# A state-space block on one core: the gates of the last two groups move behind the scan, with the norm's scaling

## The chip, the cores and the metric

The kernel runs on one core of a Trainium2 chip. The time is the device time of one execution in microseconds (us). The time before is the median of three runs: 3396.68 us (3396.28 to 3397.22).

## The reference

Input x has 2048 tokens of 1024 channels, all in float32. After a layernorm over the channels (xn), the output is x + mixer(xn) + lora(xn). The lora part is a dense 1024x1024 layer and a routed low-rank one. The mixer matters here:

```
proj = xn @ in_proj_w.T                 # gate 4096 | x 4096, B 1024, C 1024 | dt 64
xBC  = silu(causal_conv4(x, B, C))      # four taps per channel
state = state * dA_t + dtx_t (x) B_t    # 64 heads of 64, 8 groups of 8 heads, 128 states
y_t  = state @ C_t + D * x_t
yn   = y * rsqrt(mean(y*y over the 512 channels of a group) + eps) * norm_weight
out  = (yn * silu(gate)) @ out_proj_w.T
```

So a group's gate (512 of the 4096 gate channels) and a group's root of the mean square meet y only at the end, just ahead of the output projection.

## The kernel before

Channels lie on partitions and tokens along the free axis. The two halves of the sequence (s = 0, 1; 1024 tokens each) and, within a half, two blocks of 512 tokens are the units of work.

*Products.* The input projection is computed by Strassen-like block products: two channel tiles form a `pair` (L488) that takes seven products in place of eight; one product is four matmuls of 128x128 by 512 columns, which the profile counts as eight. All pairs stand in one stream, `in_pairs` (L609): for each half and group three pairs for x, B, C, then, for groups from 2*NO on, two pairs for the gate (`g..`); at the end the pairs of the dense layer (`b..`). With NO = 3 these are groups 6 and 7. `stored` (L561) evicts a quarter of a pair and sends it to DRAM (`raw_d`, `gate_d`); the gate's quarters pass through Silu.

*Scan.* 32 blocks (half, group, half of the half) of four chunks of 128 tokens give 128 slots, in an order written out by hand. In each slot the program issues: one product; `scan_b` (L802) of this chunk (matmuls ps_y, ps_e, ps_st; on VectorE ecp times ps_e, the sum into xg, and the state update, whose decay GpSimd multiplies in first); `scan_a` (L740) of the next chunk in three steps (es on VectorE; ps_cb, cbm, the mask product into dab; the transposes ps_xt and the scalings xdt, xdd on ScalarE); between them the further products, with the convolution `conv` (L682) of the next block, layernorm of the second half, and sums of weights as side work. `plan` and `target` (L1075) spread the stream's products evenly over the slots. `pin` (L98) fixes the order of many VectorE instructions, and `keep_in_program_order` that of TensorE's.

*Norm.* At a block's last slot `norm_squares` (L867) squares xg on ScalarE and adds the four tiles on VectorE. In the next block's first slot `norm_mean` (L879) sums over the channels with a matmul of ones (ps_nv, PSUM bank "aux", the same as that of ps_cb), and ScalarE takes the root into `rms`; `norm_gate` (L887) takes the reciprocal (L890), scales xg by weight and root (L893), multiplies by the gate in groups 6 and 7 (L903), and stores to `y_d`.

*Gate stage.* Behind the scan, the gates of groups 0 to 5 are computed two groups at a time (an octet) by a two-level scheme: seven outer units of seven products each, 49 in place of 64, of matmuls with 256 columns (`ps_a_z`, `ps_x_z`, `ps_y_z`). `gate_units` (L1214) lists (half, octet, unit): 2 x 3 x 7 = 42. `left_two` makes weight sums on GpSimd, `oct_sums` those of an octet, `right_two` sums of activations on VectorE. As a quarter of an octet is complete, `gated` (L1299) loads y, takes Silu on ScalarE, multiplies on VectorE (L1310) and stores to `yg_d`; `later` puts its steps at given units and products.

*Output.* The output projection runs as a two-level scheme too (`ps_.._w`), with quarters loaded from `yg_d` or `y_d`.

All DMAs are issued on SyncE's queue (SP).

## Time and profile before

| | |
|---|---|
| median of three runs | 3396.68 us |
| the profiled execution, span | 3400.1 us |
| start, up to the scan's first slot | 0 to 181 us |
| scan, 128 slots | 181 to 2103 us |
| last products of the stream | 2103 to 2164 us |
| gate stage, 42 units | 2164 to 2685 us |
| output stage | 2688 to 3395 us |
| DMA | 799.38 MB, 235 GB/s |

The profiled execution is one run; the page gives no other time for it than its span, from its first to its last instruction, and what lies around the span is not in the table. Stages are told by the names of TensorE's tiles. In rows of the profile, L81 is the helper that issues every matmul and L85 the one for GpSimd; there one goes by the tile. Each float32 matmul counts as two. A matmul's duration holds its way through the array, so the pace is the distance from one to the next: 0.43 us for 512 columns.

### The profile page before, as it was taken

The page shows a single profiled execution, that of the slowest core. Times are in us where ns is not written, and L with a number is a line of the kernel's source. Part 1 is how long each engine was busy: PE and PEld are TensorE (multiplying, and loading weights), DVE is VectorE, ACT ScalarE, POOL GpSimd, SP SyncE. Part 2 cuts the span into 40 slices and gives each one's busy share as a digit, 9 for nine tenths or more (in the row PEclk, how much of TensorE's full clock was granted, in tenths as well). Part 3 has the DMA queues.
Part 4 walks back from the last instruction along what each step waited for, and adds up shares of the span by engine and source line. Part 5 has one row for each costly group of instructions (what it writes and reads, how often), then busy time and mean ns, then how long its engine had stood idle before and what let it go on. Part 6 is the DMA issues. An engine that isn't in the chain of part 4 may idle for free.

```text
span 3400.1 us, 41266 instructions
## 1 busy us (share of the span) xinstructions
PE 3344.5 (98%) x13828; PEld 2178.1 (64%) x13828; DVE 2489.8 (73%) x2688; ACT 1523.0 (45%) x4030; POOL 703.3 (21%) x499
## 2 busy tenths in 40 slices
PE   9999999999999999999999999999999999999999
PEld 7455554555555445555555554688888888888888
DVE  7479888878889988889888897455644565556554
ACT  2356666666666666666666664222222200000000
POOL 4122222222200021212112121474444100000000
PEclk9999999999999999999999999999999999999999
DMA  6657666656689988889898999677655787585654
GB/s 244 195 158 220 197 203 200 205 192 201 193 284 335 338 269 269 256 263 272 252 291 249 268 287 302 197 228 239 221 185 182 265 301 241 200 302 177 214 167 143
DMA packets 535571, 799.38 MB, mean 235 GB/s; under 512 B 34880, under 2 KB 264384, under 8 KB 531776
## 3 DMA queue, kind: packets, MB, share of 16 engines
q1 hardware_dynamic: 535360, 796.75, 72.8%
q8 instruction: 111, 1.82, 0.2%
q14 instruction: 100, 0.82, 0.1%
HBM read 546.00 MB, written 250.61 MB: 234 GB/s over the span
## 4 chain that ended last, share of the span: by engine, by line
PE 72%; DVE 14%; DMA 6%; ACT 5%; issue 3%; SPq 0%; POOL 0%; DVEq 0%; ACTq 0%; POOLq 0%
PE ps_x_x L81 10%; PE ps_x_w L81 8%; PE ps_y_x L81 6%; PE ps_a_x L81 6%; PE ps_y_w L81 5%; PE ps_a_w L81 5%; PE ps_x_z L81 5%; PE ps_y_z L81 3%; PE ps_a_z L81 3%; DVE xg L704 3%; PE ps_e L81 2%; PE ps_y L81 2%; PE ps_st L81 2%; PE ps_x_b L81 2%; DVE es L749 2%
## 5 line engine op out<-in xcount | busy, mean ns | idle before, releaser
L85 POOL TENSOR_TENSOR state<-state,tot 128x512 f32<-128x512 f32 x112 | 136.5, 1219 | 1085.0 <-PE ps_e L81 1003.3
L704 DVE SCALAR_TENSOR_TENSOR xg<-rawx,cw,xg 128x512 f32<-128x512 f32 x384 | 331.2, 870 | 9.6 <-ACT xg L698 2.3
L749 DVE TENSOR_TENSOR_SCAN es<-dab,here 128x1024 f32<-128x1024 f32 x128 | 296.1, 2313 | 10.8 <-ACT xdt L784 5.7
L81 PE MATMUL ps_x_w<-t,w 128*128 128x256 f32 x1344 | 303.8, 379 | 0.0
L767 ACT ACTIVATE ps_y<-xg,dsk 128x128 f32<-128x128 f32 x512 | 189.6, 370 | 207.3 <-DVE xg L832 182.6
L81 PEld LDWEIGHTS ps_x_w<-t,w 128*128 128x128 f32 x1344 | 255.4, 190 | 41.5 <-issue 7.4
L792 ACT ACTIVATE xdd<-xdt,es 128x64 f32<-128x64 f32 x1024 | 262.6, 392 | 1.4 <-DVE es L749 1.4
L784 ACT ACTIVATE xdt<-ps_xt,dt 128x64 f32<-128x64 f32 x1024 | 224.3, 337 | 62.7 <-PE ps_xt L105 62.7
L81 PE MATMUL ps_a_w<-q,w 128*128 128x256 f32 x896 | 202.7, 379 | 5.1 <-DMA w<-w 5.1
L1684 ACT COPY ps_x_w<-ps_a_w 128x512 f32<-128x512 f32 x28 | 16.0, 570 | 420.9 <-PE ps_a_w L81 420.9
L704 DVE SCALAR_TENSOR_TENSOR bc<-rawb,cw,bc 128x512 f32<-128x512 f32 x192 | 186.5, 977 | 20.8 <-ACT bc L698 17.3
L81 PEld LDWEIGHTS ps_a_w<-q,w 128*128 128x128 f32 x896 | 170.1, 190 | 28.8 <-issue 5.8
L81 PEld LDWEIGHTS ps_y<-dab,xdt 128*64 128x64 f32 x2048 | 112.4, 136 | 105.7 <-ACT xdd L792 83.9
L772 DVE TENSOR_TENSOR dab<-es,cbm 128x1024 f32<-128x1024 f32 x128 | 165.5, 1293 | 13.2 <-ACT cbm L760 12.8
L81 PE MATMUL ps_x_x<-op_again,s_x 128*128 128x512 f32 x384 | 172.7, 592 | 0.0
L81 PE MATMUL ps_a_x<-op_again,a_x 128*128 128x512 f32 x384 | 172.7, 592 | 0.0
L81 PE MATMUL ps_y_x<-op_again,s_x 128*128 128x512 f32 x384 | 172.7, 592 | 0.0
L81 PE MATMUL ps_x_x<-op,s_x 128*128 128x512 f32 x368 | 167.3, 598 | 0.9 <-ACT s_x L520 0.9
L81 PE MATMUL ps_y_x<-op,s_x 128*128 128x512 f32 x368 | 165.5, 592 | 0.0
L81 PE MATMUL ps_a_x<-op,a_x 128*128 128x512 f32 x368 | 165.5, 592 | 0.0
L81 PE MATMUL ps_y<-dab,xdt 128*64 128x128 f32 x2048 | 143.3, 279 | 7.6 <-ACT xdd L792 3.9
L831 DVE TENSOR_TENSOR ecp<-ecp,ps_e 128x512 f32<-128x512 f32 x120 | 81.8, 682 | 93.0 <-PE ps_e L81 88.2
(321 smaller groups left out, 6653.5 us busy)
## 6 DMA issues: line engine op xcount, KB each, us to landing
w<-w SPq DMA_DIRECT2D x196, 512.0 KB, 3.6
dab<-da_d SPq DMA_DIRECT2D x128, 512.0 KB, 6.7
raw<-ev SPq DMA_DIRECT2D x192, 256.0 KB, 4.2
a_x<-in_w_in_dram SPq DMA_DIRECT2D x168, 256.0 KB, 4.6
w<-wo SPq DMA_DIRECT2D x96, 448.0 KB, 4.8
ecp<-run_d SPq DMA_DIRECT2D x256, 128.0 KB, 5.9
y<-xg SPq DMA_DIRECT2D x64, 512.0 KB, 4.6
rawx<-raw SPq DMA_DIRECT2D x24, 1030.0 KB, 6.9
```

The costliest lines, as they stand in the source:

```text
L81: tc.keep_in_program_order(nc.tensor.matmul(*args, **kw))
L85: ins = nc.gpsimd.tensor_tensor(*args)
L704: ins = nc.vector.scalar_tensor_tensor(dst[:, i, :], raw[:, i, k : k + TB], cw[:, ti, k : k + 1], dst[:, i, :], ALU.mult, ALU.add,)
L749: ins = nc.vector.tensor_tensor_scan(es.rearrange("p h t -> p (h t)"), dab.rearrange("p h t -> p (h t)"), here, 0.0, ALU.mult, ALU.add,)
L767: nc.scalar.activation(psy[:, j, :], xg[:, j, cs], AF.Copy, scale=dsk[:, at : at + 1])
L772: nc.vector.tensor_tensor(ms, es, cbm.unsqueeze(1).to_broadcast([P, HG, Q]), ALU.mult)
L784: ins = nc.scalar.activation(xdt[:, h, :], x_t[:, h, :], AF.Copy, scale=dt_of[s][:, half * NQ + c, at : at + 1],)
L792: ins = nc.scalar.activation(xdd[:, h, :], xdt[:, h, :], AF.Copy, scale=es[:, h, Q - 1 : Q])
L831: pin(nc.vector.tensor_tensor(ecp, ecp, pse, ALU.mult))
L1684: nc.scalar.copy(px, pa)
```

## The change

NO goes from 3 to 4: the gates of all eight groups are computed in the gate stage, in 2 x 4 x 7 = 56 units. The stream holds no gate pairs, and `stored` no Silu and no delayed eviction. The norm is split. In the scan, xg is stored to `y_d` unscaled as soon as the block ends; the squares are summed over channels with the tokens on partitions (four matmuls with one column each), and a VectorE copy puts 4 values per partition into `msq`. After the last block `norm_roots` takes all roots and reciprocals at once, transposes them, and stores them to `rms_d`. In the gate stage `gated` loads y, loads the roots broadcast over the partitions (r), and scales y by weight and root on VectorE before the multiplication by the gate.

The order of a slot changes too. The second step of `scan_a` (ps_cb) comes before the slot's second product, the third (ps_xt) straight after it, and the rest of the products last; `conv` starts a slot earlier, with one or two steps in each slot. `oct_sums` of the two later octets both run in the gate stage, each in two units.

```diff
-NO = 3
+NO = 4
...
-                for q in range(2 if g >= 2 * NO else 0):
-                    t = 4 * g + 2 * q
-                    yield pair(
-                        f"g{g}_{q}", f"g_{s}_{g}_{q}", halves(w_in[t], w_in[t + 1]), ops,
-                        stored(gate_d[g], 2 * q, s, AF.Silu), s == 0,
-                    )
...
-    N_S = 5 * G - 4 * NO
+    N_S = 3 * G
...
+        nc.sync.dma_start(y_d[g][:, :, at : at + TB], xg)
...
-    def norm_mean(s, g, half):
-        y = y_of[s, g, half]
-        ps = ps_one.tile([P, TB], F32, tag="aux", name=f"ps_nv_{s}_{g}_{half}")
-        mm(ps, ones, y[:, 0, :], start=True, stop=True)
-        std = p1.tile([P, TB], F32, tag="rms", name=f"rms_{s}_{g}_{half}")
-        nc.scalar.activation(std, ps, AF.Sqrt, bias=eps, scale=1.0 / (4 * P))
...
+    def norm_sum(s, g, half):
+
+        y = sq_of.pop((s, g, half))
+        ps = ps_one.tile([P, NQ], F32, tag="aux", name=f"ps_nv_{s}_{g}_{half}")
+        for c in range(NQ):
+            mm(ps[:, c : c + 1], y[:, 0, c * Q : (c + 1) * Q], ones[:, 0:1], start=True, stop=True)
+        at = ((s * G + g) * 2 + half) * NQ
+        nc.vector.tensor_copy(msq[:, at : at + NQ], ps)
+
+    def norm_roots():
+
+        nc.scalar.activation(msq, msq, AF.Sqrt, bias=eps, scale=1.0 / (4 * P))
+        nc.vector.reciprocal(msq, msq)
+        ps = ps_one.tile([P, Q], F32, tag="aux", name="ps_roots")
+        transpose(ps, msq)
+        roots = const.tile([P, Q], F32, name="roots")
+        nc.scalar.copy(roots, ps)
+        nc.sync.dma_start(rms_d, roots)
...
+            if nxt:
+                if c == 0:
                     conv_steps = conv(*nxt)
-                parts[1] += steps(conv_steps, 1)
-                if c < 3:
                     parts[2] += steps(conv_steps, 1)
-                    tail = steps(conv_steps, 1)
+                elif c < NQ - 1:
+                    parts[1] += steps(conv_steps, 1)
+                    parts[2] += steps(conv_steps, 1)
+                else:
+                    parts[0] += steps(conv_steps, 1)
...
+            next(a, None)
             products(1, parts[1])
             next(a, None)
-            products(1, parts[2])
-            products(min(n - 3, 1), parts[3])
-            next(a, None)
-            do_put_off()
...
+            products(n - 2, parts[2])
...
+        r = gr.tile([P, 2, TB], F32, tag="gr", name=f"gr_{s}_{o}_{a}{n}")
+        nc.sync.dma_start(
+            r,
+            rows_d[s, 2 * o : 2 * o + 2, n * TB : (n + 1) * TB].unsqueeze(0)
+            .to_broadcast([P, 2, TB]),
+        )
...
+        for q in range(2):
+            for m in range(2):
+                t = 4 * (2 * o + q) + 2 * a + m
+                nc.vector.scalar_tensor_tensor(
+                    y[:, q, m], y[:, q, m], nw[:, t : t + 1], r[:, q], ALU.mult, ALU.mult
+                )
             yield
...
-            for du, n in ((1, 0), (1, 2), (1, 3), (after, 2), (after, 4)):
+            for du, n in ((1, 0), (1, 2), (1, 3), (1, 5), (after, 1), (after, 2), (after, 4)):
```

## The prediction

> **What bounds the kernel now.** I read the busy table of the page first, then busy time by stage, then one slot of the scan on the timeline, then the rows of the work that the change touches, and last the waits of TensorE and VectorE.
>
> ```profile
> PE 3344.5 (98%) x13828; PEld 2178.1 (64%) x13828; DVE 2489.8 (73%) x2688; ACT 1523.0 (45%) x4030; POOL 703.3 (21%) x499
> core 0: us, PE busy (x) PEld busy (x) DVE busy (x) ACT busy (x) POOL busy (x), PEclk, DMA share, GB/s
> 181.00:2103.00 1922.00, 1890.95 (x7529) 988.01 (x7531) 1682.66 (x1866) 1258.24 (x3603) 383.73 (x262) 1.00 0.80 248
> 2164.00:2686.00 522.00, 512.69 (x2352) 444.39 (x2350) 261.66 (x255) 146.47 (x223) 254.15 (x176) 1.00 0.62 207
> ```
>
> The first row is the page, the others are stages: 181 to 2103 is the scan, 2164 to 2686 the gate stage. TensorE has 31 us without work in the scan and 9 in the gate stage, so it sets the pace in both. But VectorE is 88% busy in the scan, and only 50% in the gate stage. The time of the change is therefore TensorE's work, plus whatever new idle time VectorE gives it. One slot shows how close the two are:
>
> ```profile
> 1622.39 1.16 PE L81 MATMUL ps_e<-bc,state 128*128 128x128 f32 x8
> 1623.38 1.02 PE L81 MATMUL ps_st<-xdd,bt 128*128 128x512 f32 x2
> 1623.59 0.69 DVE L831 TENSOR_TENSOR ecp<-ecp,ps_e 128x512 f32<-128x512 f32 x1 [2.62 <-PE ps_e L81]
> 1624.24 3.60 PE L81 MATMUL ps_y_x<-op_again,s_x 128*128 128x512 f32 x8
> 1624.91 0.68 DVE L846 TENSOR_TENSOR state<-state,ps_st 128x512 f32<-128x512 f32 x1
> 1625.51 2.28 DVE L749 TENSOR_TENSOR_SCAN es<-dab,here 128x1024 f32<-128x1024 f32 x1
> 1627.68 0.38 PE L81 MATMUL ps_cb<-bc 128*128 128x128 f32 x2
> 1631.44 0.60 PE L105 MATMUL ps_xt<-ident,xg 128*128 128x128 f32 x4
> 1635.41 1.09 PE L81 MATMUL ps_y<-dab,xdt 128*64 128x128 f32 x16
> ```
>
> (Start, duration.) A product is eight matmuls 0.43 us apart, 3.44 us. From the ps_y at 1621.37 to the next are 14.04 us: three products and 3.7 us of scan matmuls. The point to see is the order: ps_st, product, ps_cb, product, ps_xt, product. VectorE's ecp, sum into xg and state update have 7 us and more to finish before ps_xt, and ps_cb waits for none of them.
>
> ```profile
> L749 DVE TENSOR_TENSOR_SCAN es<-dab,here 128x1024 f32<-128x1024 f32 x128 | 296.1, 2313 | 10.8 <-ACT xdt L784 5.7 <-ACT xdd L792 5.0
> L890 DVE RECIPROCAL rms<-rms 128x512 f32<-128x512 f32 x32 | 106.7, 3334 | 11.7 <-ACT rms L884 11.7
> L893 DVE SCALAR_TENSOR_TENSOR xg<-xg,nw,rms 128x512 f32<-128x512 f32 x128 | 90.8, 767 | 0.0
> L81 PE MATMUL ps_nv<-sq,ones 128*128 128x512 f32 x64 | 32.7, 592 | 0.0
> DVE ecp L831 <- PE ps_e L81: 88.2, 41, 7.4
> PE ps_st L81 <- ACT xdd L792: 6.0, 11, 1.4
> PE ps_xt L105 <- DVE state L846: 5.3, 3, 2.5
> ```
>
> The fifth row is the key to the risk: VectorE waited for ps_e in only 41 of 120 slots. In the others it came to ecp late, with work queued from the slot before. The last two rows show how little of that lateness reached TensorE.
>
> **The change part by part.**
>
> *Products leave the scan.* The gate pairs of two groups are 2 x 4 pairs of 7 products: 56 x 3.44 = 192.6 us of TensorE less. The 128 slots then hold 343 products instead of 399: 87 slots of three and 41 of two (before: 113 of three, 15 of four). A slot of two lasts 14.04 - 3.44 = 10.6 us.
>
> *Gate stage grows by two octets of 49 products.* 42 units took 521.3 us (2163.7 to 2685.0), an octet of seven 86.9: +173.8 us. A two-level octet is cheaper than the 96.3 us of the same gates in one level (28 products x 3.44), by 9.4 us; this is all that TensorE gains, 18.8 us for both.
>
> *Norm in the scan.* VectorE loses 106.7 + 90.8 + 19.0 us (gate multiply) and 10.9 us of gate sums: 227 us, 1.8 us a slot, beside 1.5 us of products. ScalarE loses 62 table loads of 1.28 us and the 22 us of roots. None of this was TensorE's bound, so it is worth only the idle time it prevents. ps_nv becomes four matmuls of one column, eight weight loads: the nearest row is ps_e, eight loads in 0.97 us, against 2 x 0.43 now. 32 x 0.11 = +3.5 us.
>
> *The order in a slot, which costs most.* In the built order the products no longer lie between ps_st and ps_cb. It reads ps_st, (ps_nv), ps_cb, product, ps_xt, the rest. At each block's first slot ps_nv and ps_cb share one PSUM bank, and the reader between them is now a VectorE copy queued behind ecp, xg and state. By the slot above the state update ends 2.2 us after the start of ps_st; the copy (like the 0.16 us rows of 128x2) and a semaphore make it 2.5. ps_st and ps_nv end at 0.86 + 0.97 = 1.83. So TensorE waits 0.65 us per block, 32 x 0.65 = 21 us, and the whole lateness of VectorE comes on top. Behind the waiting copy stand es and the mask product; TensorE's queue holds everything else behind ps_cb.
>
> How late is VectorE? Its work from one ecp to the next, by the order and the rows: common part 2.05 (three of 0.68) + 2.31 + 1.29; slot 0 adds three convolution steps of bc at 0.98 (8.6 us), slot 1 three more and three of xg at 0.87 (11.2), slot 2 nine of xg (13.5), slot 3 the squares' sums 1.9 and, in the second half, four sums of wo of about 1.17 (12.2); and 0.5 for product sums in each. Against 14.04 it is on time; against 10.6 slot 2 runs 3.4 us over and slot 3 2.1. A third of the slots are such, spread evenly, so the copy comes about (3.4 + 12.7 - 14.04 = 2.1, 2.1 and 0)/3 = 1.4 us late in the second half. In the first half, with layernorm sums in place of wo, I take 0.5. These rows sum to 4% more than VectorE's busy time in the scan, so I cut to 0.9 and 0.35: 16 x 1.25 = 20 us. Where slot 2 was short, ps_xt of slot 3 also waits: it is due 4.7 us after ps_e, the state update ends 2.1 + lateness after it, so lateness over 2.6 costs; with the layernorm slots some 15 us. The sum is 56 us. Of the present 31, half of ScalarE's 18 goes with its table loads, and VectorE's share is replaced: 9 stay. Idle in the scan goes from 31 to 65: +34. Bounds: +5, if VectorE is early at every second block, and +75, if my rows are not cut and the product sums wait in its queue.
>
> *Gate stage, more VectorE work.* Four scalings per quarter at 767 ns, 16 per octet: 12.3 us on 40.6 of 86.9, so most is covered; but the sixth unit of each octet already has 10.6 to 12.4 us of VectorE in 12.6 to 14.1, and gets 3.1 more. Uncovered 1 us per octet: +8; bounds 0 and 24 (3.1 us each eight times). The broadcast of r (512 KB, like dab, 6.7 us to landing) is issued a unit's five products, 8.6 us, before its use, behind y's on SP: at nothing; a late one costs its delay up to 2 us. GpSimd's sums of the fourth octet, 16 more of 1.5 us, go under units where its own sums leave half of 12.1 us free.
>
> *One root for all* stands in TensorE's program order: copy, table load 1.28, root, reciprocal 0.95 (128x128 row of L345), transpose: +3 us once (0 to 5).
>
> **A rule of the skill against the trace.** The clock of 1.00 holds in nearly every stretch, but 690 to 700 us, after an idle gap of 2.1 us, was granted 0.83: 1.7 us lost. Three other gaps of 2.5 to 3.3 us lost nothing. Eight or so new gaps over 2 us at one in four: 8 x 1.7 / 4 = +3. The Trainium skill, "TensorE: Matmul & The Clock Gate", section "Part 1: The HAM clock gate", says that the clock falls to half only after an idle window of about 3.4 us; by it a gap of 2.1 us is harmless and this term would be 0. It speaks against any change that opens gaps; here the row shows that it can happen earlier.
>
> **Sum.** -192.6 + 173.8 + 3.5 + 34 + 8 + 3 + 3 = +32.7 us. The profiled execution has a span of 3400.1 us, 3.4 over the median of 3396.7, and I apply the difference to the median: 3429 us.
>
> **Rivals.**
> 1. *VectorE stays on time, and the change is faster.* With 1.8 us a slot off VectorE and its four slots evener, the copies come 0.65 us after need and no more: 21 + 9 idle, no growth: -192.6 + 173.8 + 3.5 - 1 + 3 = -13, so 3383. For it: VectorE's load per time falls in the scan, and 80 us of table loads go. Against: the wait for ps_e in only 41 slots, and short slots beside nine convolution steps. With a gate stage that hides its scalings, 12 us of growth in idle time bring it to zero.
> 2. *VectorE becomes the bound of short slots.* Growth +75, gate stage +24: -192.6 + 173.8 + 3.5 + 75 + 24 + 3 + 3 = +90, so 3486. For it: DVE at 88% now, product sums in its queue waiting for products. Against: a lighter sum per slot.
> 3. *Both cancel*: growth of 5 to 15 us and a gate stage that hides its scalings, 3392 to 3402.
> The change does do what it says: the built order holds eight octets and no gate pair in the scan.
>
> **Chances.** My case (growth 20 to 60, 3415 to 3455) 0.57; rival 1 0.15; rival 3 0.12; rival 2 0.16. Within 0.2% (about what a measurement of this kernel tells from no change, 6.8 us) falls most of rival 3: faster 0.15, same 0.10, slower 0.75. The range reaches halfway into rivals 1 and 2: 3390 to 3468.
>
> **What would show it.** Right: a new wait of PE ps_cb for the VectorE copy from ps_nv of 30 to 60 us in total, PE ps_xt on state above 10, a gate stage of 56 units near 703 us, a scan near 1922 - 189 + 34 = 1767. Wrong: ps_cb waiting under 15 us (rival 1), or gate units that last 13 us throughout.

## Result and the profile after

The changed kernel takes 3536.84 us (median of four runs, 3534.14 to 3538.66) beside 3396.48 us for the kernel before on the same chip: a ratio of 1.0417 (95% interval 1.0402 to 1.0432). It is slower by 140 us, where 32.7 were forecast. The profiled execution has a span of 3534.4 us, 134.3 more than that of before.

The busy row of the page, the kernel after:

```profile
PE 3371.4 (95%) x14357; PEld 2276.4 (64%) x14357; DVE 2442.2 (69%) x2733; ACT 1460.3 (41%) x3966; POOL 792.2 (22%) x555
```

Two numbers split the 134.3 us. TensorE's idle time, span less busy time, was 3400.1 - 3344.5 = 55.6 us and is 3534.4 - 3371.4 = 163.0: +107.4. Its busy time rose by 26.9 us, although by the rows of before its work fell by 15.3 (-192.6 + 173.8 + 3.5). So some 42 us are the same matmuls at half clock. The stages of the kernel after (window, length, busy time and count of each engine, granted clock, DMA):

```profile
178.00:2019.00 1841.00, 1736.95 (x7282) 932.45 (x7281) 1465.79 (x1713) 1146.25 (x3462) 359.99 (x246) 0.98 0.77 243
...
2082.00:2819.00 737.00, 695.42 (x3137) 598.47 (x3135) 443.56 (x457) 194.81 (x296) 368.40 (x248) 0.98 0.64 222
```

The first row is the scan: 104 us without work (31 before), although VectorE is less busy than before (1466 of 1841 us, 1683 of 1922 before). The second is the gate stage: 42 us without work (9 before), 737 us long instead of the 703 forecast. The clock was 1.00 in both before; 0.98 means that the scan ran 89 us and the gate stage 24 us at half speed (clock record of the trace).

What TensorE waited for, in the whole of the kernel after (total, times, longest):

```profile
PE ps_xt L105 <- DVE state L823: 46.5, 22, 9.5
PE ps_cb L81 <- DVE msq L857: 42.4, 30, 7.1
PE ps_x_z L81 <- ACT s_z L1379: 15.1, 11, 6.7
PE ps_x_z L81 <- DVE k L1361: 14.2, 6, 6.4
...
PE ps_roots L105 <- DVE msq L862: 3.6, 1, 3.6
```

The second row is the wait for the copy from ps_nv, the first the wait of the transposes for the state, 5.3 us before. By the two halves of the scan (178 to 1141 and 1141 to 2019 us) the second row falls into

```profile
PE ps_cb L81 <- DVE msq L857: 31.1, 14, 7.1
...
PE ps_cb L81 <- DVE msq L857: 11.3, 16, 2.1
```

In the second half most of these waits last 0.53 us, the price of the copy's place alone. The long ones stand in the first half: at 471, 661 and 848 us (4.8, 4.6 and 7.1 us) small instructions of the routing and of dt, lines 337 to 433, stand in VectorE's queue ahead of the copy, at 532 and 780 us (4.5 and 3.5 us) es and convolution steps.

The timeline shows how the first row's wait comes about, in a fourth slot that follows a short third one (start, duration):

```profile
944.01 6.79 DVE L681 SCALAR_TENSOR_TENSOR xg<-rawx,cw,xg 128x512 f32<-128x512 f32 x8
...
945.73 1.16 PE L81 MATMUL ps_e<-bc,state 128*128 128x128 f32 x8
...
946.73 1.02 PE L81 MATMUL ps_st<-xdd,bt 128*128 128x512 f32 x2
...
947.59 0.38 PE L81 MATMUL ps_cb<-bc 128*128 128x128 f32 x2
...
950.72 0.68 DVE L808 TENSOR_TENSOR ecp<-ecp,ps_e 128x512 f32<-128x512 f32 x1
...
952.11 0.68 DVE L823 TENSOR_TENSOR state<-state,ps_st 128x512 f32<-128x512 f32 x1
...
952.93 0.63 PE L105 MATMUL ps_xt<-ident,xg 128*128 128x128 f32 x4 [1.42 <-DVE state L823]
```

ps_e ends at 946.89, but VectorE has convolution steps of the slot before queued until 950.80 and reaches ecp 3.8 us late. The state update ends at 952.79, and ps_xt, which the new order puts one product behind ps_st, waits 1.42 us. Before, two products lay between them. Of the 46.5 us, 41.9 stand in slots that follow a short one.

The three longest of these waits are of another kind: ahead of ecp or of the state update VectorE was not busy but waited itself. Near the scan's end:

```profile
1947.66 5.28 POOL L85 TENSOR_TENSOR wo<-wo 128x512 f32<-128x512 f32 x4 [16.57 <-DMA wo<-in_w_out_dram]
...
1953.97 0.69 DVE L823 TENSOR_TENSOR state<-state,ps_st 128x512 f32<-128x512 f32 x1 [8.05 <-POOL state L85]
...
1954.71 1.12 PE L105 MATMUL ps_xt<-ident,xg 128*128 128x128 f32 x4 [9.52 <-DVE state L823]
```

The state's decay stood on GpSimd behind sums of wo that waited for their load. In the slots from 1032 and 1094 us (ps_xt waits 4.85 and 6.29 us) a convolution step of bc, ahead of ecp in VectorE's queue, waited 3.8 and 10.4 us for ScalarE, and weight sums stood between it and ecp. The second one:

```profile
1100.24 2.33 DVE L681 SCALAR_TENSOR_TENSOR bc<-rawb,cw,bc 128x512 f32<-128x512 f32 x3 [10.39 <-ACT bc L675]
```

These three make 20.7 of the 46.5 us.

### The profile page after: what moved, and what is told of

The parts are those of the page before. It is cut to its first block, busy times and chain, and to the rows that moved or that the text cites. A ratio compares the mean times of both kernels' runs of the same rounds, so it can differ in the third digit from the quotient of the medians.

```text
span 3534.4 us, 42377 instructions
## 1 busy us (share of the span) xinstructions
PE 3371.4 (95%) x14357; PEld 2276.4 (64%) x14357; DVE 2442.2 (69%) x2733; ACT 1460.3 (41%) x3966; POOL 792.2 (22%) x555
## 4 chain that ended last, share of the span: by engine, by line
PE 61%; DVE 17%; DMA 9%; issue 5%; ACT 5%; POOL 2%; SPq 1%; DVEq 0%; POOLq 0%; ACTq 0%
PE ps_x_x L81 9%; PE ps_x_w L81 8%; PE ps_a_x L81 6%; PE ps_y_x L81 5%; PE ps_a_w L81 5%; PE ps_y_w L81 5%; PE ps_x_z L81 5%; DVE xg L681 4%; PE ps_y_z L81 3%; PE ps_a_z L81 3%; DVE es L726 2%; PE ps_e L81 2%; PE ps_y L81 2%; PE ps_x_b L81 1%; DVE dab L749 1%
## 5 line engine op out<-in xcount | busy, mean ns | idle before, releaser
L85 POOL TENSOR_TENSOR state<-state,tot 128x512 f32<-128x512 f32 x112 | 128.1, 1143 | 1082.4 <-PE ps_e L81 960.9
L681 DVE SCALAR_TENSOR_TENSOR xg<-rawx,cw,xg 128x512 f32<-128x512 f32 x384 | 323.1, 853 | 7.1
L681 DVE SCALAR_TENSOR_TENSOR bc<-rawb,cw,bc 128x512 f32<-128x512 f32 x192 | 171.3, 893 | 36.0 <-ACT bc L675 33.6
L749 DVE TENSOR_TENSOR dab<-es,cbm 128x1024 f32<-128x1024 f32 x128 | 175.9, 1375 | 18.0 <-ACT cbm L737 14.3
L465 POOL TENSOR_TENSOR s_x<-a_x,a_x 128x512 f32<-128x512 f32 x48 | 72.4, 1507 | 400.8 <-PE ps_y_x L81 295.9
```

Of the source, the lines that this page charges most:

```text
L85: ins = nc.gpsimd.tensor_tensor(*args)
L465: nc.gpsimd.tensor_tensor(t[what], t[x], t[y], alu)
L681: ins = nc.vector.scalar_tensor_tensor(dst[:, i, :], raw[:, i, k : k + TB], cw[:, ti, k : k + 1], dst[:, i, :], ALU.mult, ALU.add,)
L749: nc.vector.tensor_tensor(ms, es, cbm.unsqueeze(1).to_broadcast([P, HG, Q]), ALU.mult)
```

## The experiments

Four questions: which part of the scan's idle time is the slot's order and which the short slots; whether gaps alone cost the clock; what lengthens the gate stage; and whether the parts can be mended. "Scan idle" is the length of the scan less TensorE's busy time in it, from windows cut at each run's own stage ends. All kernels start from the kernel after unless told otherwise; the kernel before took 3394.85 to 3397.52 us beside them. Short slots are those of two products, long ones those of three and four. Times are medians of four runs, e5 and e9 single ones; stages and waits are those of the one profiled run, whose time was the lowest of the four in e13 (3494 us) and at the upper end in e3, e17 and e18 (3538, 3509 and 3532 us).

### The scan: order or short slots

**e1_norm_late.** Moved:

```diff
-            if c == 0 and prev:
-                norm_sum(*prev)
...
             products(n - 2, parts[2])
+            if c == 0 and prev:
+                norm_sum(*prev)
```

> The changed kernel with one edit: the sum of squares (ps_nv and its VectorE copy) stands at the end of a block's first slot, behind its products, instead of between ps_st and ps_cb. Theory (the order opens the gaps: ps_cb waits for the copy): the 42.4 us that ps_cb waits for the copy fall below 5, a few half-clock stretches go with them, ps_xt's 46 us on the state stay or grow by 10 at most; 3537 becomes 3480 to 3505. Rival (VectorE is simply too slow for slots of two products): the time comes back at ps_xt on state and at ps_e, idle in the scan stays above 90 us, and the time above 3520.

Measured: 3504.25 us (ratio 1.0325, 1.0309 to 1.0342). The wait of ps_cb for the copy is gone; TensorE's waits in this run have two others:

```profile
PE ps_xt L105 <- DVE state L823: 58.0, 26, 13.5
...
PE ps_nv L81 <- ACT std L291: 12.0, 4, 4.7
```

So the copy's place was worth some 32 us of time. But scan idle fell by only 20 us, to 84 (the rest is TensorE's busy time, 11 us less, with the clock): part of the lateness moved to ps_xt, and ps_nv now meets the layernorm's sums in the same PSUM bank.

**e2_old_order.** The order of before in all slots:

```diff
             next(a, None)
-            next(a, None)
             products(1, parts[1])
             next(a, None)
             products(n - 2, parts[2])
+            next(a, None)
```

> The changed kernel with the slot's order of before: ps_st, product, ps_cb, the other products, ps_xt, in slots of two products too. Theory (order): the waits of ps_cb on the copy and of ps_xt on the state fall below 15 us together, scan idle goes from 104 to 25-45 us and its half clock from 89 to under 25 us; with the clock, 3537 becomes 3415 to 3450. Rival (two or three products a slot leave VectorE too little time): the same idle time turns up at ps_y or ps_e, scan idle stays over 70 us and the time over 3490.

Measured: 3497.49 us (1.0285, 1.0256 to 1.0315). Scan idle 72 us: the rival's case. By slots, idle in long slots fell from 84 to 26 us (29 in the slots of three before), but in the 41 short ones it rose from 20 to 47. There ps_xt stands right behind ps_cb, and from ps_cb to the next ps_y ScalarE has one product where it had two:

```profile
PE ps_y L81 <- ACT xdt L761: 23.6, 8, 7.5
...
PE ps_y L81 <- ACT xdd L769: 10.6, 7, 3.2
```

**e8_mid_order.** The old order in slots of three, the new one in slots of two:

```diff
-            next(a, None)
-            products(1, parts[1])
-            next(a, None)
-            products(n - 2, parts[2])
+            if n > 2:
+                products(1, parts[1])
+                next(a, None)
+                products(n - 2, parts[2])
+                next(a, None)
+            else:
+                next(a, None)
+                products(1, parts[1])
+                next(a, None)
+                products(0, parts[2])
```

> The changed kernel with the old order (ps_st, product, ps_cb, product, ps_xt) in the 87 slots of three products and its own order in the 41 slots of two. In e2 the old order took idle time in slots of three from 84 to 26 us but raised that of the short ones from 20 to 47. Theory (each kind of slot wants its own order): 26 + 20, scan idle 40 to 55 us, scan half clock under 55 us, time 3445 to 3475. Rival (lateness is only carried from slot to slot): scan idle 65 us or more, time 3490 or more.

Measured: 3511.84 us (1.0340, 1.0325 to 1.0356), scan idle 77 us. The two halves did not add up: slots of three stood at 47 us instead of 26. The rival held: the short slot ahead hands its lateness on.

**e4_before_no4.** The kernel before with four octets (and the sums' stores late, as in e3):

```diff
-NO = 3
+NO = 4
...
-            products(1, parts[2])
+            products(min(n - 2, 1), parts[2])
```

> The kernel before with the gates of all eight groups moved behind the scan (NO = 4, so that slots hold two or three products), but its own slot order, its own norm in the scan (reciprocal and scaling on VectorE, roots on ScalarE) and no scaling in the gate stage; the sums' stores stand late as in e3. Theory (order is what costs, not the number of products): 19 us fewer products, scan idle 30 to 60 us, little half clock: 3385 to 3425. Rival (short slots): VectorE has 1.8 us a slot more here than in the changed kernel, so scan idle above 100 us and the time over 3470.

Measured: 3491.29 us (1.0281, 1.0266 to 1.0296). The scan's window:

```profile
178.00:2007.00 1829.00, 1725.28 (x7091) 915.60 (x7088) 1654.20 (x1837) 1228.11 (x3545) 368.35 (x246) 0.99 0.79 244
```

1829 - 1725.28 = 103.7 us idle with the order and the norm of before: short slots alone, with the norm of before, bring as much idle time as the whole change. Theory (order) fell here. Against e2, which has short slots and the old order too, the lighter norm is worth some 31 us of idle time; the new order takes them back.

**e7_three_octets** and **e12_three_old.** The gate pairs of groups 6 and 7 are back in the stream; e12 has e2's order as well:

```diff
-NO = 4
+NO = 3
...
+                for q in range(2 if g >= 2 * NO else 0):
+                    t = 4 * g + 2 * q
+                    yield pair(
+                        f"g{g}_{q}", f"g_{s}_{g}_{q}", halves(w_in[t], w_in[t + 1]), ops,
+                        stored(gate_d[g], 2 * q, s), s == 0,
+                    )
```

> The changed kernel with NO = 3: the gate products of groups 6 and 7 are back in the scan, so slots hold three or four products as before, but slot order and norm are those of the change. Left out: these two groups' Silu, gate multiply and norm scaling. Theory A (the order opens the gaps): ps_cb waits on the copy 25 to 45 us and ps_xt on the state 20 to 45 us as in the changed kernel, scan idle 70 to 100 us, time 3450 to 3500. Theory B (slots of two products open them, since ScalarE and VectorE do not finish in 10.6 us): ps_cb under 25, ps_xt under 10, scan idle under 50 us, half clock in the scan under 25 us, time 3395 to 3440.

> e7 (NO = 3, three or four products a slot, the changed norm; Silu, gate multiply and scaling of groups 6 and 7 left out) with the old slot order. It fills the fourth field: new norm, old order, long slots. Theory (order and slot length add up): e7's 50 us of scan idle less the 32 of ps_cb, 18 to 30 us, half clock under 8 us, time 3405 to 3430. Rival (the new norm itself opens gaps): scan idle 40 us or more, time above 3440.

Measured: 3456.32 us for e7 (1.0180, 1.0161 to 1.0199), 3431.65 us for e12 (1.0107, 1.0092 to 1.0122). e7's waits:

```profile
PE ps_cb L81 <- DVE msq L864: 31.8, 31, 5.5
...
PE ps_xt L105 <- DVE state L830: 9.1, 6, 3.8
```

Neither pure theory held: ps_cb's wait stayed (order), ps_xt's all but went (short slots). With e12 the four fields are full (scan idle, us; time):

| | old order | new order |
|---|---|---|
| long slots (NO = 3) | e12: 28.8; 3431.7 | e7: 50.1; 3456.3 |
| short slots (NO = 4) | e2: 72.3; 3497.5 | after: 104.1; 3536.8 |

The order costs 21 to 32 us of idle time, the short slots 44 to 54; the short slots are the larger part. All four fields have the earlier start of `conv`. Waits of VectorE at bc for ScalarE come to 15 to 25 us of the scan in each of them, to 2.6 in the kernel before; no run tests this start by itself. (The times of the two rows differ by the gate stage too.) e12 is still 35 us behind the kernel before: 20 of them are its gate stage (542 us against 522), and its scan ran 24 us at half clock where under 8 were expected.

**e10_lean_conv.** One convolution tap less:

```diff
-                for k in range(1, KW):
+                for k in range(1, KW - 1):
```

> The changed kernel without the last tap of the convolution (left out: one of three multiply-adds of each tile, six of 0.87 us per block, 1.3 us of VectorE a slot; nothing else moves). Theory (VectorE's lateness in slots of two products): ps_xt on state falls from 46 to under 20 us, ps_cb on the copy to 20-28, scan idle from 104 to 45-65, its half clock from 89 to under 45 us, time 3537 to 3450-3480. Rival (the order alone sets the waits, however light VectorE is): scan idle stays above 85 us and the time above 3515.

Measured: 3502.20 us (1.0311, 1.0295 to 1.0328), scan idle 77 us, between the two cases. The waits tell why:

```profile
PE ps_cb L81 <- DVE msq L857: 41.9, 31, 5.8
...
PE ps_xt L105 <- DVE state L823: 22.8, 4, 11.6
```

With 153 us less VectorE time in the scan, ps_xt's wait halves, and ps_cb's does not move. What went from ps_xt is VectorE's lateness; of what is left, 11.6 us is again one wait for the decay on GpSimd. The second is the place of the copy, behind three instructions that need ps_e and ps_st: 0.53 us a block, in e7 too, and on top of it, in the first half above all, what stands ahead of the copy in VectorE's queue (31.6 us of waits in the first half, 10.4 in the second), much of it the routing's instructions, which this edit leaves as they are.

**e15_short_first.** All together:

```diff
-            n = target(slot) - done
+            if c == 0:
+                whole = target(slot + 3) - done
+            n = whole // 4 + (whole % 4 > (3, 2, 0, 1)[c])
```

with e1's place for `norm_sum`, e8's order and e14's gate stage.

> The changed kernel with all that the runs point to: the slots of two products are the first of each block (VectorE has 8.6 us of work there against 11 to 13.5 in the others), with nine more in second slots; they keep the new order, the slots of three have the old one; the sum of squares stands at its slot's end; gate stage as e14. Theory (short slots cost where VectorE has more work than the slot lasts): scan idle 104 to 25-45 us, its half clock under 30 us, the time 3425 to 3455; still behind the kernel before, since the gate stage and the clock take more than the 19 us of products saved. Rival (any short slot carries its lateness on): scan idle 60 us or more, time 3465 or more.

Measured: 3526.41 us (1.0389, 1.0372 to 1.0406), scan idle 76 us: by the numbers the rival. Its gate stage, built as e14's, took 754 us and lost part of the gain. But the scan is two different halves: in the second half of the scan idle fell to 16 us (34 in the kernel after, 5 in e12), in the first it was 61. There ps_nv at the end of the short slot waited 19.4 us for the layernorm's roots, and ps_xt 19.2 us for the state. That short slots are harmless where VectorE has little is thus borne out only where no layernorm runs.

### The clock: gaps made on purpose

**e5_gaps.** In the output stage of the kernel before, behind a unit's first product:

```diff
                     nc.scalar.copy(px, pa)
+                    held = w_ready[0][:, 0, 0:4, :]
+                    for _ in range(1 + (7 * t + units.index(i)) % 7):
+                        nc.scalar.copy(held, held)
```

> The kernel before, with one gap made on purpose in each of the 28 units of the output stage: behind the unit's first product ScalarE, after its copy of that product's sum, copies a part of the next product's weights onto itself once to seven times (0.58 us each by the ScalarE rows of the gate stage), and the next product waits for that. TensorE is otherwise without gaps there, so the clock record answers for each length alone. Theory (a gap near or over 3 us costs the clock): gaps under 2 us are followed by a half clock in at most 1 of 8, those over 3 us in at least 10 of 12, each by 3.4 us or more of half clock (1.7 us or more lost). Rival (the clock fell in the changed kernel for another reason, its many small matmuls): at most 3 of the 28 gaps are followed by one.

Measured: the output stage of 718 us has 9.9 us idle, as before: the copies depended on the weights alone and were put ahead of the product. No gaps, no answer.

**e9_gaps_held.** The same with the copies held behind the evicting copy:

```diff
-                    nc.scalar.copy(px, pa)
+                    ins = nc.scalar.copy(px, pa)
...
-                        nc.scalar.copy(held, held)
+                        one = nc.scalar.copy(held, held)
+                        behind(one, ins)
+                        ins = one
```

> As e5, whose gaps did not come about (the copies had been put ahead of the product that they were to follow): now each of ScalarE's one to seven copies of the next weights is held behind its copy of the first product's sum. By the 0.58 us rows the gaps are about 1.4 to 4.9 us, four of each length, in the output stage. Theory (gap length decides): under 2 us at most 1 of 8 followed by a half clock, over 3 us at least 10 of 12, 3.4 us or more of half clock each; some 12 to 18 half stretches in all. Rival (another reason): at most 3 of 28.

Measured: 28 gaps as planned, four each of 1.19, 1.90, 2.49, 3.14, 3.79, 4.44 and 5.09 us. Three of them on TensorE's timeline (in brackets the gap ahead of the row and what ended it):

```profile
2715.91 5.41 PE L81 MATMUL ps_y_w<-t,w 128*128 128x256 f32 x16 [1.90 <-ACT w L1687]
...
2806.97 6.43 PE L81 MATMUL ps_y_w<-t,w 128*128 128x256 f32 x16 [3.79 <-ACT w L1687]
...
2904.55 3.72 PE L81 MATMUL ps_y_w<-t,w 128*128 128x256 f32 x16 [1.19 <-ACT w L1687]
```

and windows around these three gaps (columns as in the stages above; the second last but one is the clock):

```profile
2713.50:2716.91 3.41, 1.51 (x8) 1.01 (x7) 3.31 (x3) 1.72 (x3) 0.00 (x0) 1.00 1.05 393
2716.91:2720.32 3.41, 3.41 (x10) 2.70 (x9) 0.70 (x1) 0.00 (x0) 0.00 (x0) 0.50 1.03 398
2802.25:2805.66 3.41, 0.93 (x5) 0.48 (x3) 2.29 (x1) 2.34 (x5) 0.00 (x0) 1.00 0.94 309
2805.66:2809.07 3.41, 2.10 (x5) 1.74 (x6) 0.00 (x0) 1.23 (x2) 0.00 (x0) 0.50 0.67 198
2809.07:2812.48 3.41, 3.41 (x9) 2.69 (x9) 0.00 (x0) 0.00 (x0) 0.00 (x0) 0.50 0.42 161
2901.24:2904.65 3.41, 2.22 (x11) 1.62 (x9) 2.91 (x3) 1.10 (x2) 0.00 (x0) 1.00 1.03 357
2904.65:2908.06 3.41, 3.41 (x16) 3.02 (x17) 3.33 (x2) 0.00 (x0) 0.00 (x0) 1.00 1.00 373
```

All 24 gaps of 1.90 us and more were followed by a half clock, the four of 1.19 us by none; 109 us of half clock in all. A gap of 1.90 us took 3.41 us of half clock, one of 3.79 us two such stretches. So gaps alone do it, without small matmuls, and earlier than theory had it. (All four gaps of 1.90 us lay within one window of the grid described at the end; in the kernel after two gaps of 1.97 and 1.98 us, at 711 and 646 us, cost nothing.) The stage grew by 140 us from its 715: 87 us of gaps and some 53 us of slow clock.

### The gate stage

**e3_stores_late.** The store step of the sums comes later:

```diff
-                for u, n in ((2 * k, 4), (2 * k + 1, 2), (2 * k + 1, 6)):
+                for u, n in ((2 * k, 4), (2 * k + 1, 2), (2 * k + 2, 3)):
```

> The changed kernel with one edit in the gate stage: the store step of GpSimd's operand sums of octets 3 and 4 is issued four products later (behind the third product of the next unit), so that SP has sent the next loads of y before it waits for GpSimd. Theory (SP's queue: y's load stands behind a store that waits for GpSimd): VectorE no longer waits for y, the six long units fall to about 13 us, the gate stage goes from 737 to about 705 us, the half clock in it from 24 to under 8 us, and 3537 becomes 3500 to 3512. Rival (VectorE's scalings, 3.1 us in a unit, are the cost): the gate stage stays above 725 and the time above 3525.

Measured: 3527.83 us (1.0397, 1.0378 to 1.0416), gate stage 745 us. By the numbers it is the rival, but the edit did not do what it was meant to: SP still waited 87 us for GpSimd at these stores (83 in the kernel after).

**e6_scale_late.** The scalings stand later:

```diff
-            for du, n in ((1, 0), (1, 2), (1, 3), (1, 5), (after, 1), (after, 2), (after, 4)):
+            for du, n in ((1, 0), (1, 2), (1, 3), (after, 1), (after, 2), (after, 3), (after, 4)):
```

> The changed kernel with one edit in the gate stage: VectorE's four scalings of a quarter stand three to four products later, all in the unit after next, so that none of them waits for y ahead of the sums of the unit before. Theory (a scaling whose y has not landed holds up the sums behind it in VectorE's queue): the wait of ps_x_z on k (14 us) and the six long units shrink, gate stage 737 to 705-718, time 3510 to 3522. Rival (3.1 us of VectorE work in crowded units is the cost, wherever it stands): the sixth and seventh units of an octet lengthen instead, gate stage 728 or more, time 3530 or more.

Measured: 3538.30 us (1.0419, 1.0404 to 1.0435), gate stage 742 us: the rival's numbers, and the theory's missed. But VectorE waited 72 us for y, longer than the 63 of the kernel after, and SP 92 us for GpSimd instead of 83, so the edit did not take that wait away.

**e11_pool_stores.** GpSimd issues the sums' stores (`queue` is `nc.gpsimd` for the sums of the gate stage):

```diff
-            nc.sync.dma_start(to[what], src)
+            queue.dma_start(to[what], src)
```

> The changed kernel with the 32 stores of the operand sums in the gate stage issued by GpSimd itself, behind its sums, so that SP's queue never waits for them; nothing else moves (e3 only moved that wait: SP still waited 87 us for GpSimd). Theory (y is late because SP stands at these stores): VectorE's waits for y fall from 63 to under 30 us, the long units shrink, gate stage 737 to 705-718, time 3508 to 3522. Rival (the scalings' own time, or y's transfers, are the cost): gate stage 730 or more, time 3528 or more.

Measured: 3526.70 us (1.0389, 1.0372 to 1.0406), gate stage 736 us. By the numbers the rival again, in its stage. SP no longer waits for GpSimd, but for the buffer of the next sums, whose loads it issues (10 us in the kernel after; window 2082 to 2400), and VectorE's wait for y fell only to 55 us:

```profile
SPq L886 <- DMA s<-ws: 63.2, 14, 15.1
```

The wait had moved once more.

**e13_no_sums.** Without the eight sums of the gate stage:

```diff
-            for k in range(8):
-                gen = oct_sums(gt, 2 + k // 4, k % 4)
-                for u, n in ((2 * k, 4), (2 * k + 1, 2), (2 * k + 1, 6)):
-                    later(u, n, lambda g=gen: next(g))
...
-                src = s_d[o][i][:, q]
+                src = s_d[o % 2][i][:, q]
```

> The changed kernel without GpSimd's operand sums of octets 3 and 4 in the gate stage, with their loads and stores (left out: these sums; the units of octets 3 and 4 read those of octets 1 and 2 in their place). e3, e6 and e11 only moved the wait of SP for GpSimd. Theory (the sums' loads and stores on SP make y late, and VectorE's scaling waits for y ahead of the next sums): the six long units go, all units are like those of the second pass in the changed kernel (35 units, 0.5 us over 12.09 each): gate stage 737 to 700-708, half clock there under 8 us, time 3500 to 3512. Rival (3.1 us of scalings in a unit are the cost): gate stage 725 or more.

Measured: 3501.24 us (1.0311, 1.0287 to 1.0335). The stage:

```profile
2075.00:2780.00 705.00, 685.31 (x3137) 592.26 (x3135) 426.41 (x457) 194.62 (x296) 302.33 (x216) 1.00 0.62 210
```

705 us with the scalings in it, at a clock of 1.00: with the scalings there, the sums of octets 3 and 4 cost 32 us, 22 of idle time and 10 of clock. Neither of the two is dear alone: by 521.3 + 173.8 the stage would last 695 us without both, with the scalings 705, with the sums alone (e4, stores late) 712; with both it is 737. And waiting for y is not what went: VectorE still waited 47.9 us for y in this stage (62.7 in the kernel after).

**e14_scale_z.** z is scaled in place of y, and r is loaded ahead of y, in a step of its own at `(0, 3)`:

```diff
-                    y[:, q, m], y[:, q, m], nw[:, t : t + 1], r[:, q], ALU.mult, ALU.mult
+                    z[:, q, m], z[:, q, m], nw[:, t : t + 1], r[:, q], ALU.mult, ALU.mult
```

> The changed kernel with the scaling applied to the gate z instead of y, and the root's rows loaded a unit earlier: VectorE does the same work at the same places, but no scaling waits for y; only the last multiply does, three to four products later. Theory (it is the wait for y ahead of the k sums, not the scalings' time): gate stage 737 to 708-718 (e4, without scalings and with the same sums, had 712), ps_x_z on k under 6 us, time 3508 to 3520. Rival (scalings' time): 730 or more, time 3528 or more.

Measured: 3551.83 us (1.0463, 1.0437 to 1.0488), gate stage 751 us: worse than either case. The early load of r waited on SP 76 us for its buffer, held by a scaling that now waits for Silu. The edit made a new wait and decides nothing.

**e16_no_adds** keeps the sums' loads and stores, **e17_no_transfers** their additions; both read `s_d[o % 2]` as e13 does:

```diff
-                gen = oct_sums(gt, 2 + k // 4, k % 4)
+                gen = oct_sums(gt, 2 + k // 4, k % 4, lambda *args: None)    # e16
...
+            def sums_only():                                                 # e17
+                a11, a12, a21, a22 = (held[:, j] for j in range(4))
+                add(a22, a21, a12, ALU.add)
+                add(a21, a11, a12, ALU.subtract)
+                add(a22, a21, a11, ALU.subtract)
+                add(a21, a12, a11, ALU.subtract)
+            for k in range(8):
+                later(2 * k + 1, 2, sums_only)
```

> As e13 (705 us of gate stage without the sums), but the sums' loads and stores stay and only GpSimd's 32 additions are left out (the stores carry the loaded quarters; octets 3 and 4 read the operands of octets 1 and 2). Theory A (SP's queue and the transfers): gate stage 720 us or more. Theory B (GpSimd's additions: SP's stores wait for them, and VectorE runs slower beside them): 703 to 712, time 3500 to 3512.

> As e13, but GpSimd's 32 additions stay, on a tile loaded once, and the sums' other loads and all stores are left out, so that nothing on SP waits for them. Theory A (SP's queue): gate stage 703 to 712. Theory B, in the part that VectorE runs slower beside GpSimd, or that the additions delay the units' own operands on GpSimd: 720 or more. If both e16 and e17 come out near 705, it is the stores on SP that wait for the additions, neither alone.

Measured: 3509.73 us for e16 (1.0335, 1.0320 to 1.0351), 3506.25 us for e17 (1.0322, 1.0306 to 1.0337). The gate stage of e16, without the additions:

```profile
2076.00:2795.00 719.00, 691.60 (x3137) 596.01 (x3135) 426.25 (x457) 195.15 (x296) 304.68 (x216) 0.99 0.65 219
```

and of e17, with the additions alone:

```profile
2077.00:2795.00 718.00, 691.23 (x3137) 595.47 (x3135) 448.16 (x457) 195.01 (x296) 364.36 (x248) 0.99 0.60 206
```

Against 705 us the transfers alone cost 14 us, the additions alone 13; together they make 32. The two small numbers are near the noise: the four runs of e13 lie between 3494 and 3511 us, and by the medians the transfers cost 8 us and the additions 5. That neither part alone makes the 32 us is clear of it: by the medians both together make 36. And the third busy column shows a part of how: VectorE's same 457 instructions take 426 us without GpSimd's 32 additions and 448 beside them.

**e18_spread.** A sum every two and a half units:

```diff
-                for u, n in ((2 * k, 4), (2 * k + 1, 2), (2 * k + 1, 6)):
+                for u, n in ((5 * k // 2, 4), (5 * k // 2 + 1, 2), (5 * k // 2 + 2, 3)):
```

> The changed kernel with the eight operand sums of the gate stage spread over 20 units instead of 16 (one every two and a half units, store step in the unit after the additions). Theory (the sums come too densely for SP and GpSimd): long units shrink to 13-17 us, gate stage 737 to 715-728, time 3516 to 3530. Rival (density does not matter, each sum costs its 4 us): 733 to 745, time 3530 or more.

Measured: 3521.31 us (1.0360, 1.0343 to 1.0377); gate stage 731 us, 6 less than in the kernel after, from the slowest of the four runs; the time fell by 16. Between the cases: density is a part, the smaller one.

No run points to a version that beats the kernel before: the best ones that compute everything are e4 with 3491 and e2 with 3497 us.

## Why the prediction was right or wrong

**Sign and kind of wait: right.** The change is slower, ps_cb waits for the copy from ps_nv, ps_xt for the state, as forecast; e1 and e10 show the two apart.

**The wait of ps_cb: the sum right by luck.** It was 42.4 us where the working had 21 + 20 = 41. The place alone was 0.53 us a block (0.65 taken). But the lateness on top was put at 0.35 us a block for the first half and 0.9 for the second, and it is the other way round: 31.1 us of waits stand in the first half (16 forecast), 11.3 in the second (25 forecast). In three of the first half's waits, 16.5 us together, it was the instructions of the routing and of dt, which the working's sum of a slot does not hold.

**Products, roots: right.** ps_roots waited 3.6 us (3 forecast). The gate stage without the sums of octets 3 and 4 took 705 us against 703: the scalings cost 10 us over 521.3 + 173.8, where 8 was taken.

**Failed: the term for ps_xt, "with the layernorm slots some 15 us".** It is 46.5 us, and with it scan idle grew by 73 us, from 31 to 104, where 34 was taken between bounds of 5 and 75. The step that erred prices the lateness of the state update from sums of VectorE's own work, averaged over slots. TensorE pays slot by slot, behind short slots above all (41.9 us), and 20.7 us of the wait are three cases in which VectorE itself waited, for ScalarE and for GpSimd; no term stood for that. For the same reason "the order in a slot, which costs most" is wrong: the fields show short slots at 44 to 54 us and the order at 21 to 32.

**Failed: the clock, "eight or so new gaps over 2 us at one in four ... = +3".** It was about 42 us. The kernel after has 18 gaps over 2 us, 17 of them followed by a half clock that lasts 3.4 to 10 us. All three factors were too small: before, four gaps were over 2 us, so 14 are new where eight were taken; one in four came from three harmless gaps of one trace, which by the grid described below each lay across two windows (0.94 + 1.59, 1.77 + 0.86 and 1.64 + 1.70 us); and 1.7 us is the price of the shortest stretch.

**Failed: "GpSimd's sums of the fourth octet go under units ...: at nothing" and "issued a unit's five products before its use ...: at nothing".** e13 puts the sums of octets 3 and 4 at 32 us beside the scalings, and e16 and e17 show that both their transfers and their additions are needed for it. Two chains are seen in the kernel after. In the first, SP's queue stands at a store that waits for GpSimd, y's load is issued behind it, VectorE's scaling waits for y, and the sums into k that TensorE's bank waits for (14.2 us) stand behind that scaling. From its windows 2082 to 2400 and 2078 to 2820:

```profile
SPq L895 <- POOL ws L85: 82.6, 32, 12.7
```

```profile
DVE gy L1269 <- DMA gy<-y: 62.7, 23, 6.8
```

The second is as long, 15.1 us, and goes over ScalarE:

```profile
2210.77 2.83 DVE L1269 SCALAR_TENSOR_TENSOR gy<-gy,nw,gr 128x512 f32<-128x512 f32 x2
...
2213.52 3.35 DVE L1279 TENSOR_TENSOR c<-c,k 128x2048 f32<-128x2048 f32 x1
...
2216.90 1.06 ACT L1264 ACTIVATE c<-c 128x1024 f32<-128x1024 f32 x1 [8.12 <-DVE c L1279]
...
2220.01 3.75 PE L81 MATMUL ps_x_z<-op_again,la 128*128 128x256 f32 x8 [6.66 <-ACT s_z L1379]
```

Silu waits for a sum that stands behind the scalings on VectorE, and the copy into s_z, which frees TensorE's bank, stands behind Silu on ScalarE. In e13 this wait falls to 2.4 us, that for k only to 11.2. The edits e3, e6, e11 and e14 went at the first chain, and each time SP waited for something else or as long as before; so the chains are seen, the price of the sums is measured by leaving them out, and no single link is shown to be the cause.

**Rivals.** Rival 2 (VectorE the bound of short slots, 3486) had sizes near those measured: growth +75 (73 measured) and gate stage +24 (33 us of new idle time there). With 42 for the clock in place of its 3, its +90 become +129 of the measured +134. Its mechanism is borne out in part only, since some of the longest waits were not VectorE's work. It got 0.16 because VectorE's load falls in the change; the load said nothing about single slots.

Against the forecast, then, some 39 us are missing in the scan's idle time, 39 in the clock and 25 in the idle time of the gate stage.

## What to carry to other kernels

Price a change that thins out TensorE's stretches by its shortest stretch against the longest queue of the engine behind it, not by averages, and count what that queue itself waits for: here VectorE lost 217 us of scan work and TensorE still waited more. In this kernel a new gap of some 2 us or more on TensorE counted twice, as a rule: once as idle time and once as the half clock that follows. Work moved "under" other engines' slack brings its DMA issues into one in-order queue; follow what stands behind each of them.

## What the hardware showed

*The clock goes by fixed windows.* In six traces (after, e1, e2, e4, e7, e9) all 113 half-clock stretches begin on a grid of 3.4133 us (none off it by over 6 ns) and last 3.41 us or a multiple (the last of each trace is cut off by its end). Cutting TensorE's records by this grid: behind a full-speed window with under 1.0 us idle the next was never slow (0 of 5728), with 1.0 to 1.8 us in 7 of 116, with 1.8 to 2.0 in 12 of 28, with 2.0 or more in 88 of 89. A slow window was followed by another in 8 of 115 cases with under 0.8 us idle and in 50 of 50 above. That explains why a gap of 2 or 3 us may cost nothing (it can lie across two windows, as one of 3.58 us at the start of e9's output stage did), and why two shorter gaps that add up to 2 us within one window can cost one (0.99 and 1.19 us ahead of the half clock at 879 us in e2). The Trainium skill, "TensorE: Matmul & The Clock Gate", section "Part 1: The HAM clock gate", gives the same free-running window of 3413 ns, and the grid agrees; the reading that a whole window must be idle, on which the prediction's aside rested, does not: 1.9 us of it was enough.

*VectorE is slower beside GpSimd's additions.* The scalings of the first units (two inputs in SBUF), in the kernel after (2082 to 2340 us):

```profile
L1269 DVE SCALAR_TENSOR_TENSOR gy<-gy,nw,gr 128x512 f32<-128x512 f32 x44 | 43.7, 1029 | 43.1 <-DMA gy<-y 37.3 <-DMA gr<-rms_d 5.8
```

and in e13, without the sums of octets 3 and 4 (2075 to 2338 us):

```profile
L1269 DVE SCALAR_TENSOR_TENSOR gy<-gy,nw,gr 128x512 f32<-128x512 f32 x49 | 41.0, 871 | 20.9 <-DMA gy<-y 20.8
```

1029 against 871 ns, and 767 in the scan of before, which the prediction used. In e13 GpSimd still makes the units' own sums beside them (302 us busy in the stage); whether these make the step from 767 to 871 no run shows. The Trainium skill, "SBUF — State Buffer", section "Who interferes with whom", says that a VectorE instruction with two inputs in SBUF contends with a GpSimd instruction that reads SBUF; these rows and the 22 us between e16 and e17 agree.
